# A planned two-layer kernel: maxima kept in PSUM, norms' scaling on GpSimd, another calibration, and a new plan

## The chip, the cores and the metric

The kernel runs on one core of one Trainium2 chip. Five engines work side by side, each through its own instructions in order: TensorE (PE, with its weight loads PEld), VectorE (DVE), ScalarE (ACT), GpSimd (POOL) and SyncE (SP), which here issues the DMAs. The metric is the device time of one execution in microseconds (us), lower is better; before the change the median of three runs is 2052.18 us (2049.89 to 2052.8).

## The reference, cut to what matters

An input of 16 sequences of 256 tokens, 128 wide, goes through four blocks, each followed by `x = layernorm(x + block(x))`, all in float32:

```python
# layer 0, attention: 16 heads of 64
scores = einsum('bid,bjd->bij', q, k) * scale ; probs = softmax(scores)
# layer 0, feed-forward: route each token to one of 64 tiles, then a small spline
idx_float = sigmoid(scores / (temperature + 1e-6)) * (K - 1)      # K = 8 knots
idx_low = clip(int(idx_float), 0, K - 2) ; t = idx_float - idx_low
gate = knots[idx_low] + t * (knots[idx_low + 1] - knots[idx_low])
cluster_idx = argmax(cluster_gates) ; tile_idx = cluster_idx * 8 + argmax(sel_gates)
h = gelu(xf @ compress_w1 + compress_b1) ; comp = tanh(h @ compress_w2 + compress_b2)
# layer 1, attention: a linear one and a window of 64, joined by a gate
# layer 1, feed-forward: causal attention with normed q and k, then 8 gated experts
logits = where(causal, einsum(q, k) * QK_SCALE, -1e9) ; attn = softmax(logits)
moe = einsum('bse,bsed->bsd', gate, exp_out)
def _layernorm(x): return (x - mean(x)) / sqrt(var(x) + 1e-5)
```

## The kernel before

The 4096 tokens are cut into 8 groups of 512 (`NG`, `NJ` = 4 tiles of 128 tokens). Each group passes five stages: `stage_a` (first attention), `stage_b` (routing and spline), `stage_c` (linear and window attention), `stage_d` (causal attention and the expert gate), `stage_e` (experts). The groups overlap: while one is in its experts, the next are in earlier stages.

What sets the order on every engine is a planner, the class `Plan`. The stages don't issue instructions; they add tasks with `W.add(engines, cost, fn, r, w, ...)`: the engines that may run it, its price in ns on each, the buffers and marks that it reads (`r`) and writes (`w`), a due time `at`, an activation table, a `mode` (for TensorE, which part of the array its matmuls use: `f` the whole, `r` half the rows, `c64` half the columns, `c32` a quarter). `line` then picks again and again the task that can begin earliest, ties going to the earlier due time, and gives it buffers from fixed slots (`SLOTS`); there are four PSUM banks `p` for general use and two double banks `s` for scores. The prices of handovers (`LAG`, `OWN`), of table loads (`SWITCH`) and of a change of TensorE's mode (`DRAIN`, `CHANGE`) come into the start that it works out. Before that, `order` moves the due times of some tasks by random draws, one for each seed in `SHIFTS`; so the list of seeds and the prices together decide the order of all five engines. The order is final when the program is built; on the chip, semaphores do the rest.

The parts that the change touches, with the lines of before:

- `layernorm`: `bn_stats` (L604) and `bn_aggr` (L606) on VectorE; `root` on GpSimd (an addition, L610, and a power of −1/2, L614); then for each of 4 tiles of 128x128 a `tensor_scalar` that subtracts the mean and multiplies by the root (L622), on VectorE, or for the last norm of the last group on either. It is used in nine places per group.
- `transposed` (L636): four transpositions on TensorE, which wait for a norm, and a copy out.
- `pair`: the two heads of a pair. Scores into a double bank `s`; for the causal stage a mask is added (L673) and two maxima are taken (L682), written negated into a small SBUF tile `nm`, and multiplied by the keys' and queries' scales (L688); for the first attention one maximum does it (L692). Then ScalarE's exponentials with their sums (L711), VectorE's reciprocal (L718), GpSimd's division of the probabilities (L724, two instructions per head), TensorE's transpositions (L739) and a copy into `pt` (L588 on ScalarE, L590 on VectorE).
- `calibrate` (L873 to L896): a sigmoid by exponential and reciprocal, then the index by counting the steps that it passes, a one-hot of it, two table look-ups by product and sum, and the interpolation: 14 operations on VectorE. `first_max` (L906 to L910) makes the one-hot of the greatest. Each runs twice per group.
- `stage_b`: the scores (`sig`, 72 columns) and, later, the compression: `cw1` on `xT` with 32 rows of result (two passes of 512 columns), GELU with the bias on ScalarE (L962), a row of ones on GpSimd (L961), four small matmuls with `cw2` and the bias (two passes each), tanh (L970).
- `affine` (L1014) and single operations on GpSimd, among them the power of 16 columns in `rsqrt` (L1245).

All matmuls are issued by `mm` (L582); a float32 matmul shows as two records in the trace, a transposition as one.

Of the kernel before, what the change touches and what calls it, by code (L numbers as in the profile page):

```python
# [19 lines left out]
P = 128  # L20
# [81 lines left out]
class Plan:  # L102
# [8 lines left out]
    DRAIN = {"f": 100.0, "r": 195.0, "c64": 146.0, "c32": 165.0}  # L111
# [5 lines left out]
        72001, 104156, 158749, 530219, 618053, 867777, 115380, 1030831, 989703, 546070, 867203, 1020542,  # L117
        440858, 716864, 404846, 553536, 738754, 252182, 763753, 1033961, 742976, 662468, 1007155, 374721,
        287652, 121074, 240952, 134554, 461306, 437169, 690937, 676638, 1020922, 458402, 49049, 425176, 337599,
        243636, 394575, 649096, 974137, 232709, 861174, 342919, 731733, 719060, 691337, 1023417, 819468,  # L120
        601854, 501550, 284153, 760214, 880644, 792285, 462964, 362091, 653994, 42940, 529699, 485669, 518648,
        870924, 683956, 555652, 517353, 499298, 1039459, 75286, 524333, 291772, 465085, 40128, 225186, 323275,
        127574, 743151, 399925, 37448, 567053, 109381, 874519, 486892, 656078, 172055, 234007, 730312, 376075,
        148921, 235818, 367343, 961445, 501333, 853590, 556562, 991016, 725078, 930218, 550528, 467149, 308565,
        46851, 435626, 1000905, 373725, 1043976, 182609, 703188, 235794, 584618, 1018433, 26678, 491212,
        866682, 593224, 967203, 605009, 931059, 548320, 917182, 99498, 701869, 93350, 1024544, 994491, 425711,
        507606, 60437, 609782, 717114, 384252, 963773, 608330, 512485, 668156, 301218, 423758, 383202, 102253,
        716784, 1036658, 20379, 885232, 262474, 245451, 855069, 469770,
# [52 lines left out]

    def order(self):
# [22 lines left out]
    def line(self):  # L205
# [4 lines left out]
        table, burst, nburst, mode = None, None, {}, "f"  # L210
        for t in self.tasks:
            if t.burst is not None:
                nburst[t.burst] = nburst.get(t.burst, 0) + (1 if t.eng == "S" else 0)
# [10 lines left out]
        while done < len(self.tasks):  # L224
            best = None
            avail = {c: sorted(x for x in v if x is not None) for c, v in slots.items()}
            for e, ts in cand.items():
                pick = None
                for t in ts:
# [20 lines left out]
                    if e == "P" and t.mode != mode:  # L250
                        choice += self.CHANGE
                        start += self.DRAIN[t.mode]
# [16 lines left out]
            end = start + t.cost[t.eng.index(e)]  # L269
            free[e] = start if e == "D" else end  # L270
            if e == "P":
                mode = t.mode
# [29 lines left out]
def kernel(ctx: ExitStack, tc: tile.TileContext, a: dict, out: bass.AP):  # L302
# [73 lines left out]
    sraw = load("sraw", a["L0_ffn_signatures_raw"], [NT, D])  # L376
# [3 lines left out]
    cw1 = load("cw1", a["L0_ffn_compress_w1"], [D, COMP_H])  # L380
    cb1 = ctile("cb1", [COMP_H, 1])
    nc.sync.dma_start(out=cb1, in_=a["L0_ffn_compress_b1"].rearrange("(p o) -> p o", o=1))
    cw2 = ctile("cw2", [COMP_H + 1, 2])
    nc.sync.dma_start(out=cw2[:COMP_H, :], in_=a["L0_ffn_compress_w2"])
    nc.sync.dma_start(out=cw2[COMP_H : COMP_H + 1, :], in_=a["L0_ffn_compress_b2"].rearrange("(o c) -> o c", o=1))
# [64 lines left out]
    sig = ctile("sig", [P, NT + NCL])  # L450
    rtemp = ctile("rtemp", [P, 1])
    dknots = ctile("dknots", [P, NK - 1])
    steps = ctile("steps", [P, NK])
    back = ctile("back", [P, NK])

    def setup_b():
        W.at = 0.5
        qp, sp = W.buf("k1", "qpos"), W.buf("p", "sgps")

        def signs():  # L460
            qpos, qneg = qp()[:NT, :D], qp()[:NT, D:]
            V_.tensor_scalar(qpos, sraw, 0.3, None, ALU.is_gt)
            V_.tensor_scalar(qneg, sraw, -0.3, None, ALU.is_lt)
            V_.tensor_sub(qpos, qpos, qneg)
            V_.tensor_sub(qpos, qpos, sraw)
            V_.tensor_add(qpos, qpos, sraw)

        W.add("V", 800, signs, r=[late], w=[qp])
        W.add("P", 110, lambda: nc.tensor.transpose(sp()[:, :NT], qp()[:NT, :D], ident[:NT, :NT]), r=[qp], w=[sp])
        cs = W.buf("m", "csum")  # L470

        def clusters():
# [5 lines left out]
            V_.tensor_sub(sig[:, NT:], csum, cneg)  # L478
            V_.tensor_scalar(rtemp, temp, 1e-6, None, ALU.add)
            V_.reciprocal(rtemp, rtemp)  # L480
            V_.tensor_sub(dknots, knots[:, 1:], knots[:, : NK - 1])
            V_.tensor_copy(steps, steps_i)
            V_.tensor_scalar(back, steps, -float(NK), None, ALU.add)

        made((steps_i, 0), 150, lambda: nc.gpsimd.iota(steps_i, pattern=[[1, NK]], base=0, channel_multiplier=0))
        W.add("V", 1200, clusters, r=[sp, steps_i], w=[cs, ready_b])
# [15 lines left out]
    def setup_c():  # L502
        W.at = 0.6
        pad, pr = W.buf("k1", "pad"), W.buf("p", "prb")
        W.add("P", 110, lambda: nc.tensor.transpose(pr()[:WH, : 2 * HALF + 1], rb, ident[: 2 * HALF + 1, : 2 * HALF + 1]), r=[late], w=[pr])
# [63 lines left out]
    def pe(n, cols=P, count=1, passes=2):  # L569
        return count * passes * max(0.84 * n, 0.87 * cols)  # L570
# [4 lines left out]
    def scl(n, count=1):  # L575
        return count * (60 + 0.84 * n)
# [15 lines left out]
    def layernorm(o, z, name, after=(), js=range(NJ), own=False, last="V"):  # L592


        if own:
            for j in js:
                layernorm(o, z, name, after, [j], last=last)
            return
# [20 lines left out]
        for j in js:  # L619
            W.add(  # L620
                last, (257, 392) if last == "VG" else 257,
                lambda e="V", j=j: (nc.gpsimd if e == "G" else nc.vector).tensor_scalar(  # L622
                    o(J, d=D)[:, j, :], z(J, d=D)[:, j, :], mv()[:, 2 * j : 2 * j + 1], rs()[:, j : j + 1],
                    ALU.subtract, ALU.mult,
                ),
                r=[*zs, mv, rs] if o is not z else [mv, rs], w=[(o, ("j", j))],
            )

    def transposed(o, z, name, scale=None, shift=None, after=()):
# [8 lines left out]
        W.add("P", pe(P, count=NJ, passes=1), turn, r=[z, *after], w=[tp], hold=[o])  # L638
# [5 lines left out]
    def pair(pi, qT, kT, causal, rq, un=0):  # L644
# [24 lines left out]
        if causal:  # L669
# [7 lines left out]
            )  # L677
            for qc in range(2):
                c0, nk = col[qc]
                W.add(  # L680
                    "V", dve(2 * nk),
                    lambda qc=qc, c0=c0, nk=nk: nc.vector.tensor_reduce(  # L682
                        nm()[:, :, qc], sps(S2, a=2)[:, :, c0 : c0 + nk], AX.X, ALU.max, negate=True
                    ),
                    r=[sps], w=[(nmx, qc)],
                )
            rqp = lambda: rq("p (b i m) -> p i m b", n=16, b=2, i=2)[:, pi, 2 * un : 2 * un + 2, :]
            W.add("V", 70, lambda: nc.vector.tensor_tensor(out=nm(), in0=nm(), in1=rqp(), op=ALU.mult), r=[rq], w=[nmx])  # L688
# [10 lines left out]
        for par in range(2):  # L699
# [29 lines left out]
            W.add("G", (802 if causal else 910,), lambda norm=norm: norm("G"), r=[sm], w=[pb])  # L729
# [14 lines left out]
            W.add("P", 40 + pe(P, count=ncol // P, passes=1), turn, r=[pb], w=[tps, chain[1]], hold=[pt])  # L744
# [45 lines left out]
    def stage_a(g):  # L790
# [10 lines left out]
            w=[xx],  # L801
# [62 lines left out]
    def small(name, n, fn, r=(), w=(), eng="V"):  # L864
        W.add(eng, (60 + 1.05 * n) if eng == "V" else (60 + 1.8 * n), fn, r=r, w=w)

    def calibrate(score, deps, name):

        n = NJ * 8
        zz, at, low = W.buf("m", "zz"), W.buf("m", "at"), W.buf("m", "low")  # L870
        V = nc.vector

        small(name, n, lambda: V.tensor_scalar(zz(A8, n=n, b=8), score(), rtemp, -87.0, ALU.mult, ALU.max), r=deps, w=[zz])  # L873
        W.add("S", 100, lambda: act(zz(n=n), zz(n=n), AF.Exp, scale=-1.0), w=[zz], table="exp")
        small(name, n, lambda: V.tensor_scalar(zz(n=n), zz(n=n), 1.0, None, ALU.add), w=[zz])
        W.add("V", 60 + 6.9 * n, lambda: V.reciprocal(at(n=n), zz(n=n)), r=[zz], w=[at])
        small(name, n, lambda: V.tensor_scalar(at(n=n), at(n=n), float(NK - 1), None, ALU.mult), w=[at])
        ge = W.buf("k1", "ge")
        K6, K7 = [P, n, NK - 2], [P, n, NK - 1]
        ge6, ge7 = (lambda: ge("p (a b) -> p a b", n=n * 6, b=6)), (lambda: ge("p (a b) -> p a b", n=n * 7, b=7))  # L880
        small(name, n * 6, lambda: V.tensor_tensor(
            out=ge6(), in0=at(n=n).unsqueeze(2).to_broadcast(K6), in1=steps[:, 1 : NK - 1].unsqueeze(1).to_broadcast(K6), op=ALU.is_ge), r=[at], w=[ge])
        small(name, n * 6, lambda: V.tensor_reduce(low(n=n), ge6(), AX.X, ALU.add), r=[ge], w=[low])
        small(name, n * 7, lambda: V.tensor_tensor(
            out=ge7(), in0=low(n=n).unsqueeze(2).to_broadcast(K7), in1=steps[:, : NK - 1].unsqueeze(1).to_broadcast(K7), op=ALU.is_equal), r=[low], w=[ge])
        got = []
        for nm, tab in (("kl", knots[:, : NK - 1]), ("dk", dknots)):
            pick, r = W.buf("k1", "pick"), W.buf("m", nm)
            p7 = lambda pick=pick: pick("p (a b) -> p a b", n=n * 7, b=7)
            small(name, n * 7, lambda p7=p7, tab=tab: V.tensor_tensor(out=p7(), in0=ge7(), in1=tab.unsqueeze(1).to_broadcast(K7), op=ALU.mult), r=[ge], w=[pick])  # L890
            small(name, n * 7, lambda p7=p7, r=r: V.tensor_reduce(r(n=n), p7(), AX.X, ALU.add), r=[pick], w=[r])
            got.append(r)
        gate = W.buf("m", "gate")
        small(name, n, lambda: V.tensor_sub(gate(n=n), at(n=n), low(n=n)), r=[at, low], w=[gate])
# [677 lines left out]
```

## Time and profile before

| what | value |
|---|---|
| median of the runs | 2052.18 us |
| span of the profiled execution | 2045.3 us |
| instructions in it | 45696 |
| matmul records | 16394 |
| HBM read, written | 41.89 MB, 2.88 MB |
| DMA over the span | 23 GB/s |
| mean granted TensorE clock | 0.996 |

The profile is of one execution, taken by the hardware; its span runs from the first instruction of the program to the last, and no other time of that execution is known. Lines with `|` are groups of instructions: line, engine, operation, what is written from what, shapes, count, then busy time in us and the mean ns of one, then the idle time of the engine before them and who ended it. In the view of waits, a line names who waited, for whom, and three numbers: us in total, times, longest. In the view of one source line, the three numbers before the comma are the shortest, the median and the longest ns.

### The profile page before, as it was taken

Reading aid. Unit: us, or ns where it says so; the run is one execution under the profiler, and the core shown is the slowest. Engines: PE = TensorE matmul, PEld = TensorE weight load, DVE = VectorE, ACT = ScalarE, POOL = GpSimd, SP = SyncE. Lnnn points to the kernel's source line nnn. Section 1 sums busy time; section 2 is a strip of 40 time slices with the busy share of each in tenths; the row PEclk is TensorE's granted clock in tenths of the full one; section 3 lists DMA queues with packets and bytes.
Section 4 is the critical chain, followed back from the end, with each engine's and each line's share of the span. In section 5 each row is a group of like instructions: output and inputs, shape, how many; then the busy total and the mean of one; then the engine's idle time right before and its main releaser. Section 6 shows DMA issues by size and latency. Waiting matters only on the chain.

```text
span 2045.3 us, 45696 instructions
## 1 busy us (share of the span) xinstructions
PE 1982.4 (97%) x16394; PEld 1525.4 (75%) x16394; DVE 1544.3 (76%) x4219; ACT 1337.8 (65%) x4249; POOL 1099.5 (54%) x1662
## 2 busy tenths in 40 slices
PE   8999999999999999999999999999989999999987
PEld 6777777877776777777777687867777777777765
DVE  6898979889887687279988588856896497576542
ACT  4556666867776686456586568656787587567542
POOL 4435655867665285047665349623764395366321
PEclk9999999999999999999999999999999999999999
DMA  5200000000001100200000100011001100100111
GB/s 138 43 1 1 2 1 2 2 2 1 2 2 37 47 2 20 65 22 1 1 2 6 52 27 12 1 47 37 7 2 36 48 2 17 47 27 17 58 37 57
DMA packets 69970, 47.71 MB, mean 23 GB/s; under 512 B 12176, under 2 KB 60784, under 8 KB 69744
## 3 DMA queue, kind: packets, MB, share of 16 engines
q1 hardware_dynamic: 68896, 44.00, 7.7%
q8 instruction: 130, 2.13, 0.4%
q14 instruction: 96, 0.79, 0.1%
q10 hardware_dynamic: 848, 0.79, 0.1%
HBM read 41.89 MB, written 2.88 MB: 22 GB/s over the span
## 4 chain that ended last, share of the span: by engine, by line
PE 70%; DVE 18%; POOL 5%; ACT 3%; issue 2%; DMA 1%; POOLq 0%; DVEq 0%; ACTq 0%; SPq 0%
PE p L582 49%; PE s L582 10%; PE p L739 7%; POOL pb L724 2%; PE p L1182 2%; ACT pb L711 2%; DVE m L692 1%; DVE m L682 1%; DVE s L1153 1%; DVE m L1158 1%; DVE x L622 1%; DVE pt L590 1%; DVE s L673 1%; PE p L1355 1%; POOL m L614 1%
## 5 line engine op out<-in xcount | busy, mean ns | idle before, releaser
L724 POOL TENSOR_SCALAR pb<-pb,m 128x256 f32<-128x256 f32 (+1 forms) x1024 | 457.7, 463 | 556.7 <-DVE m L718 430.4
L1473 ACT ACTIVATE hid<-p,b 128x512 f32<-128x512 f32 x256 | 173.5, 688 | 225.3 <-PE p L582 223.3
L711 ACT ACTIVATE pb<-s,m 128x256 f32<-128x256 f32 x512 | 237.5, 486 | 120.4 <-DVE m L692 94.7
L739 PE MATMUL p<-ident,pb 128*128 128x128 f32 x1792 | 261.1, 278 | 9.0 <-POOL pb L724 2.5
L711 ACT ACTIVATE pb<-s,m,m 128x128 f32<-128x128 f32 (+1 forms) x512 | 256.3, 521 | 16.1 <-DVE m L688 12.5
L582 PEld LDWEIGHTS p<-w,hid 128*128 128x128 f32 x2048 | 242.7, 192 | 30.9 <-issue 28.7
L739 PEld LDWEIGHTS p<-ident,pb 128*128 128x128 f32 x1792 | 204.7, 142 | 67.2 <-POOL pb L724 29.6
L582 PE MATMUL p<-w,hid 128*128 128x128 f32 x2048 | 248.0, 275 | 0.2 <-DMA w<-in_L_ffn_w_dram 0.2
L582 PE MATMUL p<-h,w 128*128 128x512 f32 x512 | 242.3, 602 | 1.6 <-DMA w<-in_L_ffn_w_dram 0.9
L590 DVE COPY pt<-p 128x384 f32<-128x384 f32 (+1 forms) x288 | 171.4, 611 | 43.4 <-PE p L739 42.1
L1168 ACT ACTIVATE pbC<-s,m 128x96 f32<-128x96 f32 (+1 forms) x512 | 174.0, 374 | 19.9 <-DVE m L1158 14.4
L1245 POOL TENSOR_TENSOR m<-m,mhalf 128x16 f32<-128x16 f32 x64 | 185.9, 2914 | 1.9
L588 ACT COPY pt<-p 128x512 f32<-128x512 f32 (+1 forms) x224 | 118.0, 550 | 92.4 <-PE p L739 87.3
L1493 DVE SCALAR_TENSOR_TENSOR e<-p,m,e 128x128 f32<-128x128 f32 x248 | 71.5, 344 | 138.4 <-PE p L582 87.5
L692 DVE TENSOR_REDUCE m<-s 128x4 f32<-128x1024 f32 x128 | 153.3, 1217 | 23.2 <-PE s L582 21.0
L1176 POOL TENSOR_TENSOR pbC<-pbC,m 128x384 f32<-128x384 f32 (+1 forms) x128 | 119.8, 940 | 90.8 <-DVE m L1172 72.8
L582 PEld LDWEIGHTS p<-h,w 128*128 128x128 f32 x512 | 90.0, 192 | 80.7 <-issue 64.8
L718 DVE RECIPROCAL m<-m 128x2 f32<-128x2 f32 x512 | 79.1, 157 | 80.9 <-ACT pb L711 78.7
L582 PE MATMUL s<-ua,ua 64*128 64x256 f32 x1024 | 134.5, 392 | 1.7 <-ACT pb L711 1.6
L682 DVE TENSOR_REDUCE m<-s 128x2 f32<-128x256 f32 (+1 forms) x256 | 131.1, 550 | 1.3
L582 PE MATMUL p<-pt,ua 128*64 128x256 f32 x1024 | 124.6, 385 | 0.8 <-DVE c L590 0.5
L1168 ACT ACTIVATION_READ_ACCUMULATOR pbC<-s,m 128x1 f32 x512 | 115.7, 226 | 0.0
(268 smaller groups left out, 4348.1 us busy)
## 6 DMA issues: line engine op xcount, KB each, us to landing
w<-in_L_ffn_w_dram SPq DMA_DIRECT2D x128, 256.0 KB, 2.7
x<-_attn_hidden_states_dram SPq DMA_DIRECT2D x7, 256.0 KB, 5.8
out_dram<-x SPq DMA_DIRECT2D x7, 256.0 KB, 2.4
dpad<-k SPq DMA_DIRECT2D x1, 768.0 KB, 10.3
wkv<-in_L_attn_Wkv_dram SPq DMA_DIRECT2D x2, 256.0 KB
wo<-in_L_attn_Wo_dram SPq DMA_DIRECT2D x1, 512.0 KB
fqk<-in_L_ffn_Wq_dram SPq DMA_DIRECT2D x1, 512.0 KB, 5.5
fqk<-in_L_ffn_Wk_dram SPq DMA_DIRECT2D x1, 512.0 KB, 6.3
```

Of the source, the lines that this page charges most:

```text
L582: nc.tensor.matmul(o, lhsT=lhsT, rhs=rhs, start=start, stop=stop)
L588: nc.scalar.copy(o, i)
L590: nc.vector.tensor_copy(o, i)
L682: lambda qc=qc, c0=c0, nk=nk: nc.vector.tensor_reduce(nm()[:, :, qc], sps(S2, a=2)[:, :, c0 : c0 + nk], AX.X, ALU.max, negate=True),
L692: lambda: nc.vector.tensor_reduce(nm(), sps(S2, a=2).rearrange("p a (b k) -> p a b k", k=S), AX.X, ALU.max, negate=True),
L711: act(pb()[:, c0 : c0 + nk], s[:, par, c0 : c0 + nk], AF.Exp, bias=nmx()[:, 2 * par + qc : 2 * par + qc + 1], accum_out=sums()[:, 2 * par ...
L724: eng.tensor_scalar(pb()[:, c0 : c0 + nk], pb()[:, c0 : c0 + nk], sums()[:, 2 * par + qc : 2 * par + qc + 1], 1.0, ALU.mult, ALU.mult,)
L739: nc.tensor.transpose(tps()[:, at * P : (at + 1) * P], pb()[:, c0 + kc * P : c0 + (kc + 1) * P], ident)
L1168: act(pb("p (u k) -> p u k", u=4)[:, u, :nk], s8[:, hp, :nk], AF.Exp, bias=nmx()[:, hp : hp + 1], accum_out=sm()[:, u : u + 1])
L1176: G.tensor_tensor(out=w4, in0=w4, in1=sm()[:, :4].unsqueeze(2).to_broadcast([P, 4, nk]), op=ALU.mult)
L1245: lambda cs=cs: G.tensor_tensor(out=o()[:, cs], in0=ve()[:, cs], in1=mhalf[:, :16], op=ALU.pow),
L1473: W.add("S", 571, lambda ph=ph, hid=hid, ec=ec: act(hid(), ph(), AF.Gelu_apprx_tanh, bias=b1[:, ec : ec + 1]), r=[ph], w=[hid], table="gel ...
```

## The change

Six things change.

1. In `pair`, the causal stage's negated maxima are written into two unused columns of their own PSUM bank (`low`) and read from there.
2. In `layernorm`, all scalings of 128x128 go to GpSimd.
3. `calibrate` works the interpolation as a sum over 8 steps: each step's rise times the clamped distance into it; four operations of 256 elements per partition take the place of eleven.
4. `stage_b`'s scores carry 32 more columns, the compression; the bias is added on VectorE, GELU runs on 128x128, the product with `cw2` on GpSimd, its sum on VectorE. The matmuls of the compression are gone. `sraw` is loaded by a planned task into a buffer.
5. The planner's prices: a change of mode costs what leaving the old form takes (`EXIT`), and the first task after a change or a pause costs more (`COLD`, `WARM`); transpositions have a form of their own; and VectorE operations marked `port` are lengthened when they start within a GpSimd operation marked `lock`.
6. `SHIFTS` is another list of seeds (220 for 147).

```diff
-    DRAIN = {"f": 100.0, "r": 195.0, "c64": 146.0, "c32": 165.0}
+    FORM = {"t": "f"}
+    COLD = {"f": 105.0, "t": 57.0, "r": 108.0, "c64": 60.0, "c32": 22.0}
+    EXIT = {"f": 95.0, "r": 98.0, "c64": 100.0, "c32": 112.0}
+    WARM = 60.0
+    LOCK = {"lock": 1.0, "lock2": 1.0}
...
-                    if e == "P" and t.mode != mode:
+                    if e == "P" and self.form(t) != mode:
                         choice += self.CHANGE
-                        start += self.DRAIN[t.mode]
+                        start = max(start, free[e] + self.EXIT[mode])
...
+            if e == "G" and t.mode in self.LOCK:
+                held, last, piece = start, end, (end - start) / self.LOCK[t.mode]
+            if e == "V" and t.mode == "port" and held <= start < last:
+                end = max(end, held + piece * (math.floor((start - held) / piece) + 1.0))
+            if e == "P" and (self.form(t) != mode or start > free[e] + self.WARM):
+                end += self.COLD[t.mode]
...
+    NS = NT + NCL
+    sig = ctile("sig", [P, NS + COMP_H])
+    nc.sync.dma_start(out=sig[:, NS:], in_=a["L0_ffn_compress_w1"])
...
+    def turns(count=1):
+        return 109.3 * count
...
         for j in js:
             W.add(
-                last, (257, 392) if last == "VG" else 257,
-                lambda e="V", j=j: (nc.gpsimd if e == "G" else nc.vector).tensor_scalar(
...
+                "G", 345,
+                lambda e="G", j=j: norm_on(e, o(J, d=D)[:, j, :], z(J, d=D)[:, j, :], mv, rs, j),
+                r=[*zs, mv, rs] if o is not z else [mv, rs], w=[(o, ("j", j))], mode="lock",
             )
...
+            lows = object()
+            low = lambda: sps(S2, a=2)[:, :, 3 * P : 3 * P + 2]
             for qc in range(2):
...
-                        nm()[:, :, qc], sps(S2, a=2)[:, :, c0 : c0 + nk], AX.X, ALU.max, negate=True
+                        low()[:, :, qc], sps(S2, a=2)[:, :, c0 : c0 + nk], AX.X, ALU.max, negate=True
...
-            W.add("V", 70, lambda: nc.vector.tensor_tensor(out=nm(), in0=nm(), in1=rqp(), op=ALU.mult), r=[rq], w=[nmx])
+            W.add("V", 70, lambda: nc.vector.tensor_tensor(out=nm(), in0=low(), in1=rqp(), op=ALU.mult), r=[lows, rq], w=[nmx], hold=[sps])
...
+        sides(name, n * 8, lambda: V.scalar_tensor_tensor(
+            u8(), at(n=n).unsqueeze(2).to_broadcast(K8), float(NK - 1), starts.unsqueeze(1).to_broadcast(K8), ALU.mult, ALU.subtract), r=[at], w=[up])
+        sides(name, n * 4, lambda: V.tensor_scalar(up(), up(), 0.0, 1.0, ALU.max, ALU.min), w=[up])
+        sides(name, n * 8, lambda: V.tensor_tensor(out=u8(), in0=u8(), in1=rises.unsqueeze(1).to_broadcast(K8), op=ALU.mult), w=[up])
+        small(name, n * 8, lambda: V.tensor_reduce(gate(n=n), u8(), AX.X, ALU.add), r=[up], w=[gate])
...
-        W.add("P", pe(512), lambda: mm(ph()[:COMP_H, :], cw1, xT()), r=[xT], w=[ph], hold=[hT])
-        W.add("G", gps(512), lambda: G.memset(hT()[COMP_H : COMP_H + 1, :], 1.0), r=[xT], w=[(hT, 1)])
-        W.add("S", scl(512), lambda: act(hT()[:COMP_H, :], ph()[:COMP_H, :], AF.Gelu, bias=cb1), r=[ph], w=[(hT, 0)], table="gelu")
...
-        W.add("P", pe(P, count=4), squeeze, r=[hT], w=[pc], hold=[comp])
...
+        W.add("S", scl(NJ * COMP_H), lambda: act(h(n=NJ * COMP_H), h(n=NJ * COMP_H), AF.Gelu), w=[h], table="gelu")
+        W.add(
+            "G", gps(256),
+            lambda: G.tensor_tensor(
+                out=prod("p (j c k) -> p j c k", j=NJ, c=2), in0=h("p (j k) -> p j k", n=NJ * COMP_H, j=NJ).unsqueeze(2).to_broadcast(nh),
+                in1=cw2.unsqueeze(1).to_broadcast(nh), op=ALU.mult,
+            ),
+            r=[h], w=[prod], mode="lock",
+        )
```

`norm_on` with `e="G"` is `nc.gpsimd.tensor_scalar(o, z, mean, root, subtract, mult)`; `sides` is `small` with `mode="port"`.

## The prediction

> **What bounds the kernel now.** I read the page first: its busy line, its slices and its chain.
>
> ```profile
> PE 1982.4 (97%) x16394; PEld 1525.4 (75%) x16394; DVE 1544.3 (76%) x4219; ACT 1337.8 (65%) x4249; POOL 1099.5 (54%) x1662
> PE   8999999999999999999999999999989999999987
> PE 70%; DVE 18%; POOL 5%; ACT 3%; issue 2%; DMA 1%; POOLq 0%; DVEq 0%; ACTq 0%; SPq 0%
> ```
>
> TensorE is busy in every slice, and no stage has another limit. But matmul records overlap, so 97% hides bubbles. The timeline of TensorE shows the true spacing (start, length, what, how many):
>
> ```profile
> 116.84 1.10 PE L582 MATMUL p<-wo,ov 128*128 128x128 f32 x8
> 117.87 1.04 PE L582 MATMUL p<-b,cw 128*32 128x512 f32 x2
> ...
> 125.88 1.05 PE L582 MATMUL p<-cw,b 33*128 33x2 f32 x8
> 126.86 0.66 PE L739 MATMUL p<-ident,pb 128*128 128x128 f32 x4
> ```
>
> Taking off the last record's own length (276, 605, 248, 278 ns in the groups), starts lie 0.118, 0.44, 0.115 and 0.127 us apart; over the whole trace the median spacing is 0.112 us for a 128-column pass, 0.109 for a transposition, 0.216 for 256 columns, 0.429 for 512, and half that for matmuls on half the rows or columns, which start in pairs 7 ns apart. Summed over all 16394 records this is 1816 us. Entering and leaving the half-array forms costs about 0.09 and 0.15 to 0.21 us (medians of 413 such runs), 94 us in all. So TensorE has **1910 us** of work in a span of 2045.3; the other **135 us** are the head (3.6 before the first matmul), the tail (9.5 after the last one's start) and 122 us of bubbles. Some 58 us of these are bubbles of 50 to 150 ns, 722 of them; 76 us are longer ones, 154 of them. The view of waits names whom they wait for:
>
> ```profile
> PEld p L739 <- POOL pb L724: 29.6, 83, 2.2
> ...
> PE p L636 <- DVE d L622: 6.0, 2, 4.8
> ...
> POOL pb L724 <- DVE m L718: 430.4, 141, 53.0
> ```
>
> The transposition of probabilities waits for GpSimd's division, which waits for VectorE, which waits for ScalarE: a chain of latency, on engines with room.
>
> The groups by form that price the change:
>
> ```profile
> L688 DVE TENSOR_TENSOR m<-m,m 128x4 f32<-128x4 f32 x128 | 33.2, 260 | 0.5
> L622 DVE TENSOR_SCALAR x<-x,m,m 128x128 f32<-128x128 f32 x64 | 27.4, 481 | 3.5 <-POOL m L614 3.3
> L724 POOL TENSOR_SCALAR pb<-pb,m 128x128 f32<-128x128 f32 x256 | 99.3, 388 | 245.7 <-DVE m L718 176.0 <-DVE m L1318 23.9 <-PE p L739 11.5
> L622 POOL TENSOR_SCALAR e<-e,m,m 128x128 f32<-128x128 f32 x1 | 0.8, 797 | 0.1
> L688 DVE TENSOR_TENSOR m<-m,m x128: 94/157/2476, 404.1 to 1955.3; 128x4 f32<-128x4 f32 x128
> L1473 ACT ACT_TABLE_LOAD x26 | 33.4, 1283 | 0.5
> ```
>
> **The change, part by part.** The span is the only time of the profiled execution; the median of the three runs, 2052.18, lies 6.9 us above it, and I add that to every sum.
>
> **TensorE's work.** Compression leaves it: per group two 512-column passes (0.44 each) and eight passes on `cw2` (0.115 each), 1.8 us, times 8 is −14.4. The scores widen from 72 to 104 columns, 64 passes; a pass of 128 columns takes 0.112, one of 72 starts its successor after 0.11, so this costs 0 to 0.5. No form with rows or columns cut is added or dropped, but the new draws reorder everything: the orders of both programs as built hold 202 and 203 runs of half-row scores, 128 and 128 of half-column values, 82 and 81 of quarter-column ones. With the prices above the order of before sums to 1910.2 and that of after to 1896.4: **−13.8**. Nothing hides this; TensorE is the bound.
>
> **The bubbles.** In both orders I took, for each scores matmul, the TensorE work lying between its end and the first transposition of its probabilities. In the first layer that chain needs 1.22 (maximum, L692), 1.41 (two exponentials and their sums, L711), 0.16 and two L724 at 0.455: 3.7 us, plus four handovers, so a distance under 5 us has no room for a queue. There are 29 of 128 first halves under 5 us before and 17 after; medians are 6.76 and 7.52. All halves under a limit (6 us for the first layer, 7 for the windows and the causal stage) fall from 121 to 94 of 640, by 22%. The waits of transpositions and of the next scores on a bank make 68 of the 122 us, so 22% is −15. The other bound comes from the chain: VectorE loses about 145 us (norms 104, L688's waits 13, calibration 35, less 7 for compression's three new operations) of its 1544, of which 368 (18% of the span) lay on the chain, so −34; GpSimd gains 99 of 1100, with 102 on the chain, +9: together −25. Zero is a bound too, as TensorE has other work for most waits. I take **−20**, nearer the count of distances.
>
> Inside this are edits costed at nothing of their own. Calibration drops, per call, 0.24+0.48+0.35+0.46+0.85+0.75+0.82 us of VectorE for four operations of 256 (0.45 to 0.5 each by L938, L890; 0.42 the sum): 2.2 us less, 16 times. It is hidden by other groups' matmuls; uncovered, it would be worth 35. ScalarE loads 59 tables instead of 68, 9 times 1.283 is 11.5 us, and a load sits before the exponentials that the chain needs. Causal maxima go to unused columns of their own PSUM bank and are read there: L688 has median 157 but mean 260 and a worst case of 2476 ns, like L622's 481 against a median of 346. L992, the same size with one operand in PSUM, has 157 at most 158. So the long ones are waits beside GpSimd's power operation (L1245, 2.9 us), and 13 us of them end. The two reductions feeding it write PSUM instead of SBUF; L673, which writes PSUM, takes 693 for 512 columns where L682 takes 683, so at most +10 ns each.
>
> The Trainium skill speaks against the norms' move: SBUF — State Buffer, section on the two separate sides, says that VectorE and GpSimd share one pair of ports as an exclusive lock which a GpSimd instruction holds for its whole length, blocking VectorE instructions with two SBUF inputs or in a two-port mode. L688's 2476 ns agrees. By the rule the 283 moved norms add 99 us of held lock, to be set against VectorE operations that no longer ask for it; if a quarter were paid on the path, the sum would be 25 us higher.
>
> **Norms on GpSimd.** 283 scalings of 128x128 move. Each is bounded by 0.349 us (L724 of that size, start to start, one column operand) and 0.797 (the one record with two). I take 0.349, since 256 records stand against one in the crowded tail: +99 us of GpSimd, 54% to 59%; by the upper end +226, 65%. Behind them in GpSimd's queue stand the divisions L724, for which transpositions wait. The gain beside it is one handover less after L614. GpSimd's new product of 256 for compression (about 0.64, from L1176's 0.84 for 384 and 1.04 for 512) takes the place of a fill of 0.52. On SP five small loads take the place of four, at 0.31 to 0.44 of issue each, behind the inputs and weights that stage a needs; `sraw` moves to a planned load, of which only stage b's setup hears.
>
> **The end.** The last norms have no cover: PE waited 4.8 us for L622 at the last causal norm, and the tail runs 9.5 us. There GpSimd does the root and the scaling in turn; four scalings at 0.35 partly replace one handover each: 0 to +2, I take **+1**.
>
> Sum: −13.8 −20 +1 = −32.8; 2052.2 − 32.8 = **2019**. Its own range, with bubbles from −5 to −40, is 1999 to 2034.
>
> **Rivals.**
> *Only TensorE's work counts* (bubbles stay 122): −13.8 + 1 gives 2039. For it: distances under 5.5 us in second halves hardly move (10 to 9), and banks of the four shared ones are reused after the same distance (transpositions 2.45 against 2.56 median). Against: fewer tight chains.
> *GpSimd's queue becomes the wait* (slower). Place: L724 behind a group of four norms, in 71 layernorms. Price: 4 times 0.45 us if a two-column scaling takes 0.797. It decides from 18 layernorms whose whole delay of 1.8 reaches TensorE (18 times 1.8 is 33, the gain). With half of them, 36, it is +64: 2083. For: 29.6 us of waiting for L724 already, and the only row of that form. Against: GpSimd idles 430 us before L724.
> *The bubbles halve*: −61 instead of −20: 1978. For: 58 us are tiny bubbles which the new prices count for the first time. Against: as many runs of each form as before.
>
> **How the numbers follow.** Forecast 0.50, TensorE's work alone 0.23, GpSimd's queue 0.17, bubbles halved 0.10. The range 1990 to 2050 leaves out most of the third and the fourth, about 0.2. A measurement of this kernel can't tell under 0.2%, 4 us, from none. Faster: 0.50, 0.10 and 0.18 of the second, 0.78; same, the second's rest, 0.05; slower 0.17.
>
> **What would show it.** No `cw` matmuls and some 16314 records of PE; DVE near 1400, POOL near 1200; L688's successor with a mean near 160. GpSimd's norm near 370 ns and waits of `PEld` for POOL below 30 us confirm the forecast. A norm near 800, or waits for POOL above 60 us, means the slower rival. A PE clock below 0.99 would void the sum.

## The result, and the profile after

The changed kernel takes 2167.76 us (median of 4 runs, 2166.52 to 2171.02); the kernel before took 2052.49 (2049.89 to 2054.04) beside it. The ratio is **1.0568, 95% interval [1.0553, 1.0583]**: 115 us slower, where 33 us faster had been forecast. The first view to read is again the page: span, TensorE's busy line, its slices, the granted clock of each slice, and the chain.

```profile
span 2169.1 us, 45451 instructions
PE 1998.9 (92%) x16314; PEld 1533.9 (71%) x16314; DVE 1445.1 (67%) x3854; ACT 1317.8 (61%) x4236; POOL 1319.0 (61%) x1945
...
PE   6559998999999899999999998999999999999987
...
PEclk8779999999999999999999999999999999999989
...
PE 55%; POOL 23%; DVE 10%; SPq 5%; issue 3%; ACT 1%; DMA 1%; another core or an unknown queue 0%; POOLq 0%; ACTq 0%; DVEq 0%
```

Two things are new. TensorE, never under 8 tenths before except in the last slice, is half idle in the first three slices (54 us each), and there the clock falls too. And the share of GpSimd on the chain went from 5% to 23%. Two places, so two causes to look for.

**The first 130 us.** A table of windows by stage (stretch, its length, busy us and instructions of PE, PEld, DVE, ACT and POOL, then granted clock, DMA share and GB/s), before and then after:

```profile
20.00:60.00 40.00, 40.00 (x286) 31.68 (x285) 31.30 (x56) 21.11 (x79) 17.60 (x38) 0.97 0.48 109
```

```profile
20.00:60.00 40.00, 23.05 (x162) 17.80 (x162) 15.90 (x28) 15.29 (x55) 10.63 (x23) 0.80 0.05 1
60.00:100.00 40.00, 21.21 (x134) 16.91 (x134) 12.45 (x23) 6.11 (x20) 6.56 (x14) 0.76 0.06 3
```

Every engine is slack at once and the DMA moves next to nothing: 1 GB/s against 109. What holds it is in SP's timeline (start, time at the issue, what, how many):

```profile
16.07 27.52 SPq L404 DMA_DIRECT2D cw<-in_L_ffn_compress_w_dram  x2
43.63 39.00 SPq L350 DMA_DIRECT2D cb<-in_L_ffn_compress_b_dram  x1
82.67 3.46 SPq L411 DMA_DIRECT2D table<-in_L_ffn_spline_w_dram  x1
...
125.20 3.03 SPq L479 DMA_DIRECT2D sq<-_ffn_signatures_raw_dram  x1
```

The two loads of `cw2` at L404 take one column each of a 32x2 array for all 128 partitions: every second element of 4 bytes. That is 2 x 128 x 32 = 8192 pieces of one element. The next issue stands until 82.7, and `sraw` starts 109 us after the first of them. The view of DMA in the stretch 20 to 50 (packets, MB and rate; then each queue's packets, MB and share of 16 engines), of before and of after:

```profile
DMA packets 9568, 3.51 MB, mean 117 GB/s; under 512 B 5600, under 2 KB 9179, under 8 KB 9563
...
q8 instruction: 2, 0.03, 0.4%
q14 instruction: 3, 0.02, 0.2%
```

```profile
DMA packets 3188, 0.01 MB, mean 0 GB/s; under 512 B 3188, under 2 KB 3188, under 8 KB 3188
...
q1 hardware_dynamic: 3188, 0.01, 4.6%
...
cw<-in_L_ffn_compress_w_dram SPq DMA_DIRECT2D x1, 16.0 KB, 79.6
```

3188 packets in 30 us are 106 per us, one in 9.4 ns, of 4 bytes (0.01 MB); 16 KB took 79.6 us to land. In these 30 us there is no packet of the two *instruction* queues, where there were five before. Now TensorE's timeline (start, length, what, how many, and in brackets what it waited for):

```profile
40.60 2.00 PE L608 MATMUL s<-ua,ua 64*128 64x256 f32 x16
...
59.91 3.68 PE L608 MATMUL p<-pt,ua 128*64 128x256 f32 x15 [16.95 <-issue]
...
98.19 2.29 PE L608 MATMUL s<-ua,ua 64*128 64x256 f32 x9 [18.79 <-issue]
```

TensorE stops in the middle of a run of matmuls whose data is there, waits for nothing that the profile shows ("issue"), and goes on at 59.9 and 98.2, after instruction packets at 57.2 to 58.5 and at 95.8 to 96.9. The reading that fits is that it had run out of instructions: both times it goes on 1.3 us after the last of these packets has landed. Fifteen and nine matmuls after the two pauses take 0.25 us each, sixteen before them 0.125: that is the lower clock, granted at 0.50 from 59.9 to 63.6 and from 98.2 to 100.5, and at 1.00 from 40.6 to 42.6. A third pause of 25 us ends at 131, when the signs made from `sraw` arrive (L490 in the next view).

**The rest of the program.** The view of waits, for the weight loads of TensorE:

```profile
PEld p L771 <- POOL pb L756: 56.8, 112, 6.6
PEld p L490 <- DVE k L487: 25.0, 1, 25.0
PEld p L666 <- POOL d L623: 23.7, 16, 7.9
```

Transpositions of probabilities waited 29.6 us for GpSimd's division (now L756) before, 56.8 now; transpositions of normed rows (L666) wait for GpSimd's scaling. The groups by form show why:

```profile
L756 POOL TENSOR_SCALAR pb<-pb,m 128x128 f32<-128x128 f32 x256 | 97.6, 381 | 203.1 <-DVE m L750 172.0 <-DVE m L1135 11.2 <-PE p L771 9.1
...
L623 POOL TENSOR_SCALAR x<-x,m,m 128x128 f32<-128x128 f32 x64 | 50.2, 795 | 0.7
```

A scaling on GpSimd takes 0.80 us, over twice a division of the same size.

**The sum.** For every program below I took the spacings of TensorE's starts apart as in the prediction: the work at the median spacing of each form, the prices of leaving and entering forms, and what remains, the bubbles (so matmuls that run at a lower clock count as bubbles too). Before: 1816.3 of matmul work and 122.8 of bubbles. After: 1802.2 and 258.6. So the span's +123.8 is −14.1 of work, +135.8 of bubbles and 2 more of tail (9.5 to 11.5). The experiments divide the 135.8.

### The profile page after: what moved, and what is told of

Its sections match the earlier page's. It is cut to its first block, busy times and chain, and to the rows that moved or that the text cites. A ratio compares the mean times of both kernels' runs of the same rounds, so it can differ in the third digit from the quotient of the medians.

```text
span 2169.1 us, 45451 instructions
## 1 busy us (share of the span) xinstructions
PE 1998.9 (92%) x16314; PEld 1533.9 (71%) x16314; DVE 1445.1 (67%) x3854; ACT 1317.8 (61%) x4236; POOL 1319.0 (61%) x1945
## 4 chain that ended last, share of the span: by engine, by line
PE 55%; POOL 23%; DVE 10%; SPq 5%; issue 3%; ACT 1%; DMA 1%; another core or an unknown queue 0%; POOLq 0%; ACTq 0%; DVEq 0%
PE p L608 38%; PE s L608 8%; PE p L771 6%; POOL pb L756 5%; POOL m L1283 3%; POOL x L623 3%; POOL m L647 2%; SPq L350 2%; POOL pbC L1214 2%; PE p L1220 2%; POOL d L623 1%; SPq L404 1%; POOL b L1052 1%; DVE m L637 1%; POOL c L623 1%
## 5 line engine op out<-in xcount | busy, mean ns | idle before, releaser
L756 POOL TENSOR_SCALAR pb<-pb,m 128x256 f32<-128x256 f32 (+1 forms) x1024 | 454.6, 461 | 528.6 <-DVE m L750 463.1
L771 PE MATMUL p<-ident,pb 128*128 128x128 f32 x1792 | 272.8, 282 | 29.0 <-POOL pb L756 16.7
L771 PEld LDWEIGHTS p<-ident,pb 128*128 128x128 f32 x1792 | 208.1, 143 | 99.6 <-POOL pb L756 56.8
L608 PEld LDWEIGHTS p<-w,hid 128*128 128x128 f32 x2048 | 241.5, 192 | 27.3 <-issue 24.7
L608 PE MATMUL p<-h,w 128*128 128x512 f32 x512 | 242.6, 607 | 6.2 <-DVE e L1531 2.5
L608 PE MATMUL p<-w,hid 128*128 128x128 f32 x2048 | 245.4, 276 | 0.4 <-ACT hid L1511 0.2
L724 DVE TENSOR_REDUCE m<-s 128x4 f32<-128x1024 f32 x128 | 153.3, 1218 | 46.5 <-PE s L608 45.6
L608 PEld LDWEIGHTS p<-h,w 128*128 128x128 f32 x512 | 91.5, 193 | 93.7 <-issue 75.2
L608 PE MATMUL s<-ua,ua 64*128 64x256 f32 x1024 | 137.5, 397 | 20.7 <-issue 18.8
L608 PE MATMUL p<-pt,ua 128*64 128x256 f32 x1024 | 129.9, 396 | 17.0 <-issue 17.0
L714 DVE TENSOR_REDUCE s<-s 128x2 f32<-128x512 f32 (+1 forms) x256 | 140.2, 559 | 3.2
L608 PEld LDWEIGHTS s<-ua,ua 64*128 64x128 f32 x1024 | 94.7, 191 | 46.4 <-issue 29.1
```

The lines of the kernel that those rows point to most:

```text
L608: nc.tensor.matmul(o, lhsT=lhsT, rhs=rhs, start=start, stop=stop)
L714: lambda qc=qc, c0=c0, nk=nk: nc.vector.tensor_reduce(low()[:, :, qc], sps(S2, a=2)[:, :, c0 : c0 + nk], AX.X, ALU.max, negate=True),
L724: lambda: nc.vector.tensor_reduce(nm(), sps(S2, a=2).rearrange("p a (b k) -> p a b k", k=S), AX.X, ALU.max, negate=True),
L756: eng.tensor_scalar(pb()[:, c0 : c0 + nk], pb()[:, c0 : c0 + nk], sums()[:, 2 * par + qc : 2 * par + qc + 1], 1.0, ALU.mult, ALU.mult,)
L771: nc.tensor.transpose(tps()[:, at * P : (at + 1) * P], pb()[:, c0 + kc * P : c0 + (kc + 1) * P], ident)
```

## The experiments

Beside the change itself, kernels were timed in three comparisons, whose runs of the kernel before had medians of 2050.41 (the first four), 2052.56 and 2050.23 (the last two). Each ratio is to the before of its own comparison.

| kernel | median us | ratio [95%] | bubbles us |
|---|---|---|---|
| before | 2052.49 | 1 | 122.8 |
| after | 2167.76 | 1.0568 [1.0553, 1.0583] | 258.6 |
| e1_load | 2097.33 | 1.0230 [1.0215, 1.0245] | 184.4 |
| e2_norm_dve | 2103.85 | 1.0260 [1.0243, 1.0277] | 194.9 |
| e3_both | 2034.57 | 0.9922 [0.9906, 0.9938] | 121.8 |
| e4_before_strided | 2110.61 | 1.0294 [1.0278, 1.0309] | not worked out |
| e6_price | 2113.06 | 1.0293 [1.0276, 1.0310] | 195.2 |
| e7_plan_dve | 2066.76 | 1.0072 [1.0057, 1.0087] | 150.8 |
| e9_no_draws | 2064.36 | 1.0060 [1.0045, 1.0075] | 142.6 |
| e10_form | 2044.76 | 0.9975 [0.9963, 0.9986] | 130.9 |
| e12_own_draws | 2031.30 | 0.9907 [0.9893, 0.9922] | 113.5 |

**e1_load: the load of `cw2` alone mended**, as one load of 64 neighbouring elements per partition, read transposed by its one user.

```diff
-    cw2 = ctile("cw2", [P, 2, COMP_H])
-    for i in range(2):
-        nc.sync.dma_start(out=cw2[:, i, :], in_=a["L0_ffn_compress_w2"][:, i].partition_broadcast(P))
+    cw2 = ctile("cw2", [P, COMP_H, 2])
+    nc.sync.dma_start(
+        out=cw2.rearrange("p k c -> p (k c)"), in_=a["L0_ffn_compress_w2"].rearrange("k c -> (k c)").partition_broadcast(P)
+    )
...
-                in1=cw2.unsqueeze(1).to_broadcast(nh), op=ALU.mult,
+                in1=cw2.rearrange("p k c -> p c k").unsqueeze(1).to_broadcast(nh), op=ALU.mult,
```

> The changed kernel, but cw2 is loaded by one DMA of 64 contiguous elements to each partition instead of two DMAs that pick every second element (8192 pieces of 4 bytes); every engine's order is that of the changed kernel. Theory (the load blocks the start): SP issued nothing useful from 16 to 97 us, TensorE reached its 376th matmul at 131 us instead of 64, so the time falls by 60 to 70 us, to about 2100. Rival (the start would have been hidden, GpSimd sets the end anyway): less than 20 us.

2097.33: 70 us come back, as expected, bubbles fall by 74.2, and the first three slices are at 8 and 9 tenths. The three pauses were 60 of the 74.2. The waits for GpSimd stay about as they were:

```profile
PEld p L772 <- POOL pb L757: 56.2, 110, 6.5
...
PEld p L667 <- POOL d L624: 23.3, 15, 7.9
...
PE p L667 <- POOL d L624: 19.9, 12, 7.6
...
PE p L772 <- POOL pb L757: 16.8, 19, 2.5
...
PEld p L667 <- POOL c L624: 14.8, 12, 3.3
```

**e2_norm_dve: the scalings alone back on VectorE**, in the same order of tasks.

```diff
-            nc.gpsimd.tensor_scalar(o, z, mv()[:, 2 * j : 2 * j + 1], r, ALU.subtract, ALU.mult)
+            nc.vector.tensor_scalar(o, z, mv()[:, 2 * j : 2 * j + 1], r, ALU.subtract, ALU.mult)
```

> The changed kernel, but the 283 scalings of a norm are issued on VectorE, at the same places of the plan's order; the other engines keep their order. Theory (a scaling takes 0.80 us on GpSimd where the plan counts 0.345, 4 times 0.45 per norm is 1.8 us late for what waits): the bubbles after the start, about 180 us against 122 before, go back to near 120, so the time falls by 45 to 60 us, to about 2115. Rival (the new prices and draws make a worse order of themselves): less than 15 us.

2103.85: 64 us come back, somewhat more than expected, with the stalled beginning left as it is.

**e3_both: both edits together.**

> Both edits: cw2 loaded in one piece, scalings on VectorE. Theory (these two are all that went wrong): the gains add, 2040 to 2050, at or a little below the kernel before. Rival (the order is worse too): 2065 or more.

2034.57, below what either side expected, and **0.8% under before**, with an interval clear of 1. Its waits:

```profile
PEld p L772 <- POOL pb L757: 27.6, 75, 2.4
...
PEld p L667 <- DVE d L624: 10.5, 6, 5.0
...
PE p L667 <- DVE d L624: 9.3, 7, 4.7
...
PE p L772 <- POOL pb L757: 2.9, 7, 0.7
```

Against e1_load the weight loads' wait for divisions falls by 28.6, that for scalings by 27.6 (23.3 + 14.8 to 10.5). Weight loads run beside matmuls, so these numbers tell where the waits are and not what they cost. TensorE's own idle time, the sum of its rows (`PE`) in the same view, falls from 93.4 to 52.7, and the part of it that ended with GpSimd from 66.2 to 5.9. The rest of the 62.6 us of bubbles between the two fits slower matmuls: the granted clock was 0.985 in e1_load and 0.995 here, which makes some 21 us by an estimate from the two (1.5% of 2095 less 0.5% of 2030). So the 135.8 divide into 74.2 for the load, 62.6 for the scalings, and −1.0 for everything else in the change.

**e4_before_strided: the two loads put into the kernel before**, where nothing uses them (into a buffer that is written again later).

```diff
+    for i in range(2):
+        nc.sync.dma_start(out=slots["e"][0][:, i * COMP_H : (i + 1) * COMP_H], in_=a["L0_ffn_compress_w2"][:, i].partition_broadcast(P))
```

> The kernel before, with the two picking DMAs of compress_w2 added at the same place of SP's queue, into a buffer that nobody reads before stage e. Theory (the load blocks the start by itself): 55 to 75 us slower than before, 2108 to 2128. Rival (it only matters with the changed order): within 15 us of before.

2110.61, 60 us slower. The loads alone do it, without the change's other parts, and in the same way; the view of waits:

```profile
PE p L584 <- issue: 19.4, 1, 19.4
PE p L741 <- issue: 17.5, 1, 17.5
```

The pauses of 17.5 and 19.4 end at 58.3 and 96.6, 1.4 us after the last of this run's instruction packets, which come at 54.9 to 56.9 and 93.7 to 95.2.

**e5_forms: what a scaling costs by its form.** At the end of the kernel before, with nothing else running, seven forms of `tensor_scalar` on 128x128, six times each, on GpSimd and then on VectorE.

```diff
+        M, S_, A_ = ALU.mult, ALU.subtract, ALU.add
+        forms = [(1.0, 1.0, M, M), (p0, 1.0, M, M), (p0, p1, M, M), (1.0, 1.0, S_, M), (p0, 1.0, S_, M), (p0, p1, S_, M), (p0, p1, M, A_)]
+        for eng in (nc.gpsimd, nc.vector):
+            for s0, s1, o0, o1 in forms:
+                for _ in range(6):
+                    eng.tensor_scalar(fo_, fi_, s0, s1, o0, o1)
```

> The kernel before, and after its last operation six tensor_scalar of 128x128 in each of seven forms on GpSimd, then the same on VectorE: constants or columns as the two scalars, multiply-multiply, subtract-multiply, multiply-add. Theory (the second column operand costs): on GpSimd 0.37 to 0.39 us with constants or one column, 0.75 to 0.80 with two, whatever the operations. Rival (the operations cost): 0.80 in all three subtract forms, 0.39 with two columns multiplied. Rival (a neighbour's lock made it long): under 0.45 in all forms, since nothing else runs. VectorE: 0.20 to 0.28 in all.

This kernel was run once, for durations alone. GpSimd's timeline, where neighbouring forms with the same buffers share a row (constants multiplied; one, then two columns multiplied; constants subtracted and multiplied; the three others):

```profile
2049.49 2.21 POOL L1553 TENSOR_SCALAR hid<-xT 128x128 f32<-128x128 f32 x6
2051.80 6.02 POOL L1553 TENSOR_SCALAR hid<-xT,k 128x128 f32<-128x128 f32 x12
2057.91 4.28 POOL L1553 TENSOR_SCALAR hid<-xT 128x128 f32<-128x128 f32 x6
2062.30 13.46 POOL L1553 TENSOR_SCALAR hid<-xT,k 128x128 f32<-128x128 f32 x18
```

The first and third rows differ only in the first operation: 2.21 us against 4.28 for six. The typical record of each form, in ns:

| form | GpSimd | VectorE |
|---|---|---|
| two constants, multiply and multiply | 300 | 227 |
| one column, multiply and multiply | 374 | 287 |
| two columns, multiply and multiply | 450 | 346 |
| two constants, subtract and multiply | 644 | 227 |
| one column, subtract and multiply | 717 | 287 |
| two columns, subtract and multiply (a norm) | 795 | 346 |
| two columns, multiply and add | 452 | 346 |

The first two expectations were each partly wrong, and so were the 0.20 to 0.28 us for VectorE: each column costs some 75 on GpSimd, but it is the **subtraction in first place that adds 344**, and VectorE makes no difference between the two. And 795 with nothing else running is what a scaling typically took in the changed kernel: contention isn't what makes it long.

**e6_price: e1_load with the scalings priced at 795** in the planner instead of 345.

```diff
-                "G", 345,
+                "G", 795,
```

> The changed kernel with cw2 in one piece, scalings on GpSimd as in the change, but priced 795 in the plan instead of 345: a new order. Theory (GpSimd's time itself is the cost, 128 us more on the queue of the divisions): 2085 or more, near the 2097 of the same kernel at the wrong price. Rival (the wrong price is the cost, and a plan that knows makes room): 2065 or less.

2113.06 with 195.2 us of bubbles; by the ratios it is 0.6% worse than e1_load with the wrong price. That is what the theory expected, but not for its reason alone: TensorE's idle time that ended with GpSimd fell from 66.2 in e1_load to 30.3, so the plan did make room there, while its idle time in all stayed near (93.4 to 90.7). A new price also gives a new order, for which the seeds weren't drawn. This run doesn't tell what a plan at the right price with seeds of its own would reach.

**e7_plan_dve and e9_no_draws: the scalings planned on VectorE** at 257 as before, on top of e1_load; and the same with an empty list of seeds.

```diff
-                "G", 345,
-                lambda e="G", j=j: norm_on(e, o(J, d=D)[:, j, :], z(J, d=D)[:, j, :], mv, rs, j),
...
+                "V", 257,
+                lambda e="V", j=j: norm_on(e, o(J, d=D)[:, j, :], z(J, d=D)[:, j, :], mv, rs, j),
...
-    SHIFTS = (
...
+    SHIFTS = ()
```

> The changed kernel with cw2 in one piece, scalings on VectorE and also planned there (257, marked port): a new order, in which 178 of the 640 halves have a tight distance from scores to transposition against 94 in e3_both's. Theory (draws fit the plan for which they were found): slower than the 2034.6 of e3_both, 2045 to 2075. Rival (a plan with the right engine is better): 2030 or less.

> As e7_plan_dve, but with an empty list of seeds; 169 tight halves. Theory (draws are worth something only with their own plan): within 12 us of e7_plan_dve. Rival (draws help any plan): slower than it by more than 20 us.

2066.76 and 2064.36. Planned where it runs, the scaling makes a program 1.5% *slower* (by the ratios) than e3_both, which only moves it after planning; and without any seeds it is no worse. Both came out as the theory expected: the change's seeds are worth nothing under this other plan.

**e12_own_draws: e7_plan_dve with 37 seeds drawn for its own plan** (random ones, kept when the planner's own end came earlier).

```diff
-    SHIFTS = (
...
+    SHIFTS = (123963, 247028, 216123, 896726, 745462, 1035349, 486448, 834812, 230536, 436108, 214302, 769025, 406102, 374387, 948281, 806028, 1026124, 417857, 108249, 557272, 398142, 528050, 702484, 413792, 363209, 485241, 265605, 991858, 646366, 101274, 70869, 795762, 43869, 1009923, 614449, 516538, 863568)
```

> As e7_plan_dve (scalings on VectorE, planned there, cw2 in one piece), but with 37 seeds drawn anew for just this plan; 141 tight halves against 178. Theory (draws are worth something with their own plan): 20 to 35 us below the 2064 to 2067 of e7_plan_dve and e9_no_draws, so 2030 to 2045. Rival (draws are noise on the chip): within 10 us of these.

2031.30, as the theory expected: 1.5% under e9_no_draws by the ratios, and level with e3_both (the two intervals overlap). So it was seeds of its own that e7_plan_dve lacked.

**e10_form: the scalings stay on GpSimd in the cheap form**, x times r plus (−mean times r), with two small GpSimd operations more for each root, on top of e1_load.

```diff
-            nc.gpsimd.tensor_scalar(o, z, mv()[:, 2 * j : 2 * j + 1], r, ALU.subtract, ALU.mult)
+            nc.gpsimd.tensor_scalar(o, z, r, rs()[:, 2 * NJ + j : 2 * NJ + j + 1], ALU.mult, ALU.add)
...
+                nc.gpsimd.tensor_scalar(nb, mv()[:, 2 * a0 : 2 * a1].rearrange("p (j s) -> p j s", s=2)[:, :, 0], -1.0, 1.0, ALU.mult, ALU.mult)
+                nc.gpsimd.tensor_tensor(out=nb, in0=nb, in1=rs()[:, a0:a1], op=ALU.mult)
```

> The changed kernel with cw2 in one piece and scalings on GpSimd at the plan's price of 345, but as multiply-add: the product of mean and root is made negative and kept by two small operations more per norm, and each scaling is 0.452 us by e5_forms instead of 0.795. GpSimd's sum falls by 283 times 0.343, less 71 times about 0.4: 69 us net. Theory (the subtraction's time on GpSimd's queue is what costs): about two thirds of the 63 us between e1_load's 2097 and e3_both's 2035 come back, 2050 to 2070. Rival (four scalings in GpSimd's queue cost at any length): 2085 or more.

```profile
L624 POOL TENSOR_SCALAR x<-x,m 128x128 f32<-128x128 f32 x64 | 28.7, 460 | 0.7
```

460 ns instead of 795, and 2044.76, below the expected 2050 to 2070: 52.6 of the 62.8 us between e1_load and e3_both come back with the work still on GpSimd, where two thirds were expected. So most of the loss is the length of the instruction, not the engine as such; the last 10 us aren't divided.

## Why the prediction was wrong

**The step that failed most: "On SP five small loads take the place of four, at 0.31 to 0.44 of issue each".** It counted instructions, not what each one breaks into. L404 (the lines that e1_load takes out) reads `[:, i]` of an array whose last dimension is 2, so each piece is one element, and two instructions make 8192 packets of 4 bytes. They held SP for 66 us, where 0.31 to 0.44 each was counted, and cost the program 74.2 us of bubbles. The second half of that step, "`sraw` moves to a planned load, of which only stage b's setup hears", named the right listener and no price: with its issue that late, TensorE waited 25 us at the transposition L490. The warning "a PE clock below 0.99 would void the sum" came true (0.968 over the whole program), but the low clock came with the two losses: it is 0.985 in e1_load, without the load's pauses, and 0.995 in e3_both, without either.

**Second: "I take 0.349 ... since 256 records stand against one in the crowded tail".** The one record, 0.797, was the only one of the *same form*, subtract then multiply with two columns, and it was exact. The 256 were another operation. The other end of the bounds came true: 1319.0 us of GpSimd, against 1099 + 226. The sign that was named for the slower rival, a norm near 800, was there. A majority of records of another operation is no evidence. The rows should have been told apart by their operation, as they were by their shape. Another number pointed the same way and was not weighed: the Trainium skill's GPSIMD Engine Reference, section on performance versus the Vector engine, has an element-wise addition of two tensors 1.96 times as slow on GpSimd. For the scaling, which reads one tensor, the traces give 795 against 346, 2.3 times, but 300 against 227 for constants multiplied.

**The slower rival** had the right mechanism, and its size came out: "+64" if a scaling takes 0.797, against 62.6 of bubbles and 62.8 of median measured (e1_load to e3_both). That the size fits so well is partly luck: 36 layernorms was an assumption, half of 71, and the place was half right. The weight loads' waits rose by 28.6 at the division behind the scalings, as told, and by 27.6 at the transpositions of the scalings' own result, which the prediction hadn't priced; nor had it a term for the lower clock. Its 2083 also holds a gain in bubbles that never came; without that it would have been 2103, beside e1_load's 2097.

**Third: "The bubbles ... I take −20".** With both losses taken out, bubbles are 121.8 against 122.8: −1.0 where −20 was taken. The count of tight halves did fall, 121 to 94 of 640, in the order of e3_both too, and it bought nothing; the waits for the division were 27.6 and 29.6. Counts across plans point the right way only roughly: 169 and 178 halves go with 142.6 and 150.8 us, but 141 (e12_own_draws) with 113.5. In these plans the distance to the first transposition doesn't decide most bubbles.

**What held.** "TensorE's work −13.8": measured −14.1, with 16314 records as said. Without the two losses the change is worth about this: e3_both, with the scalings on VectorE, is 15.8 us under before, at 2034.6 where "only TensorE's work counts" had 2039. The tail, taken at +1, grew by 2. The causal product's mean fell from 260 to 151 ns:

```profile
L720 DVE TENSOR_TENSOR m<-s,m 128x4 f32<-128x4 f32 x128 | 19.3, 151 | 1.1
```

But the power operation (L1245) wasn't what the old one waited for. By the trace of before, all 22 records of L688 over 250 ns end 8 to 23 ns after the end of another GpSimd instruction (L1176, L1345, L724, L1014 or L1119), and none after L1245. Calibration's new operations took 0.56, 0.48, 0.42 and 0.41, together 1.87 us, within what the prediction's prices give. ScalarE loads 59 tables, as said. VectorE got 99 us lighter, not 145 (1445 against "near 1400"), and no run shows a gain from that: e10_form, with 1443 on VectorE, is 10 us behind e3_both with 1518. The ports' lock, which the prediction put at 25 us if it bit, doesn't show on VectorE: its 3854 instructions other than scalings sum to 1668.0 us in e1_load and 1667.3 in e3_both.

**What stays open.** Why the subtraction is slow on GpSimd isn't shown. That instruction loads were held back, and that TensorE stopped for want of them, is read from the times of their packets in two kernels, and what held them is not known. An addition in first place, scalings on ScalarE, and a plan with seeds of its own for e6_price or e10_form were not tried.

## What to carry to other kernels

Before costing a load at its issue, count its pieces: its elements, copies to partitions included, divided by the contiguous run in the source. Here the run was one element, and 8192 elements were 8192 packets. Price a moved operation by a record of the same operations and operand kinds on the engine that will run it, even if there is only one. And when a kernel's order comes from a search under given prices, a change of price can throw the search away, as it did in e7_plan_dve: compare orders searched equally, or the searched one may win for that reason alone.

## What the runs showed of the hardware

- Single elements of 4 bytes went at 9.4 ns each. The times of their packets are 4.6% of what 16 engines had in those 30 us, and by the trace no packet at all was under way in 12 of the 30 us. So these transfer times aren't what limits the load; how the packets were spread over the engines isn't recorded.
- Such a load stops more than its own queue: in 30 us there was no instruction packet, and TensorE stopped for 17 and 19 us with its data ready, in two different kernels. The Trainium skill's DMA: Bandwidth & Descriptors, section on queues, rings and completion order, says that an engine takes turns between its rings packet by packet; by that, an instruction load would wait for little more than the packet under way. The measured gap of 37 us between instruction packets (58.5 to 95.8) doesn't fit that, and this case doesn't show where the hold-up is.
- `tensor_scalar` on GpSimd, 128x128: 300 ns with two constants, some 75 more for each column, 344 more if the first operation subtracts. On VectorE 227, 287 and 346, with either first operation.
- After the pause of 19 us, matmuls of the same form (L608, `s<-ua,ua`) took 0.25 us instead of 0.125, with a granted clock of 0.50 while they ran.
- A VectorE product with both operands in SBUF (L688, median 157 ns) took up to 2476 ns in the kernel before, and its long records end 8 to 23 ns after a GpSimd instruction does.
